# Layer 0 of a two-layer graph network: the norm of x and its fetch tested by place in the order instead of by a counter

## The chip, the core and the metric

The kernel runs on one core of a Trainium2 chip. The time is the device time of one execution in microseconds (us). The core has five engines that run beside each other, each with its own instruction queue: TensorE (PE, matmuls; PEld is its weight load), VectorE (DVE), ScalarE (ACT), GpSimd (POOL) and SyncE (SP, which here only issues DMAs). They wait for each other by semaphores.

## What is computed

For 16 batches of 1024 nodes with 128 features, two layers with a residual each. Layer 0 is three graph convolutions whose edge weights are the adjacency times the cosine of the node features; layer 1 first thins out the adjacency row by row ("dilation") and then runs three SAGE layers with batch norms on it.

```python
# layer 0, per batch
h = relu(layernorm(x))
for i in range(3):
    h = h @ W[i] + b[i]
    nh = h / max(norm(h), 1e-12)
    h = (adj * (nh @ nh.T)) @ h
    if i < 2: h = relu(h)
x = x + h
# layer 1, per batch
h = relu(layernorm(x))
adj_d = adj * keep          # keep: every sf-th neighbour of a row is removed, rows in sequence
for i in range(3):
    agg = (adj_d @ h) / max(sum(adj_d), 1)
    o = agg @ Wr[i] + h @ Wx[i] + bS[i]
    h = batchnorm(relu(o / max(norm(o), 1e-12)))       # statistics over all batches
x = x + concat(h1, h2, h3) @ Wl + bl
```

## The kernel before

The code hands a list of operations with tiles to a framework that allots the buffers of each pool and orders every engine's instructions ahead of time: an instruction may be placed earlier than in the text where its inputs and a buffer are free. The order on each engine is then fixed.

**Two stages.** The first, to about 1740 us, runs layer 0 of all batches and the dilation beside each other. The dilation (`dilation`, `dilate`, L519 to L718) goes through eight row blocks of 128 in two halves of eight batches: SP loads adjacency rows (`an`) and the transposed keep pattern (`kl`), ScalarE and VectorE make a 0/1 pattern, a few rounds on VectorE and TensorE settle which rows are cut, a running sum along each row on VectorE (L696) ranks the neighbours, and GpSimd issues the store of the keep pattern (`kp`). Layer 0 is a generator (`layer0`), and L740 to L743 draw from it so many steps for each finished part of the dilation. The second stage, from about 1740 us to the end, is layer 1's three SAGE layers (L773 on); the change does not touch it.

**Layer 0.** A batch is an object `Batch` with a counter `l` of the convolution it is in. The list `order` (L414) has 48 places: for each pair of batches a and b it reads a, b, a, b, a, b, so that six places make one pair. The loop at L443 goes through the places i; `now` is the batch of place i, `then` that of the next, `after` that of the one after next, and `ended` a batch whose third convolution was at the place before. Each place has eight steps s, one for a block row of the symmetric matrix:

- `products` (L310): the cosines of one block row by matmuls into `pg` (two PSUM banks), and VectorE multiplies them with the adjacency and its transpose (L334, L337) into `ew`.
- `turn` (L345): transposes of the second half of `ew`, copied back by ScalarE (L355).
- `sums` and `sums_back` (L357, L373): the matmuls that sum into `po`. They run LAG = 3 steps behind, so the last step of a convolution is summed at s = 2 of the next place. There `sums_back` copies `po` to `hT` and raises `l` (L391).

Beside these steps, `then` is prepared: at s = 0 its `norm` (only in its first convolution), at s = 3 the transposes of the normed x (`enter`, also only then), at s = 4 and 5 its product with the weights (`features`), and at s = 6 `turned` and `scaled`. At s = 5 the x of `after` is fetched if `after` is in its first convolution. For `ended`, x is fetched again at s = 1, the residual is added at s = 3 (`residual`), and at s = 5 the second layer's norm is taken (`next_layer`). The last batch's residual and second norm come after the loop (L769, L770).

**The norm and the fetch.** `fetch` (L252) is one DMA of 512 KB on SP into a buffer `xb`, of which there are two. `norm` (L256) takes a buffer `tt`, of which there are two also (shared with the residual's x2 and the second layer's h0), and calls `layernorm_relu` (L136): for each of eight chunks of 128 nodes a statistic and its aggregate on VectorE (L141, L142), then a root on ScalarE (L144), a reciprocal and a small product on VectorE (L145, L147), and eight activations on ScalarE (L149) that write the result. Both conditions that decide on them ask whether the counter is 0:

```python
                    if s == 5 and after and after.l == 0:
                        after.fetch()
                    if then:
                        new = then.l == 0
                        if s == 0 and new:
                            then.norm()
```

Of the kernel before, what the change touches and what calls it, by code (L numbers as in the profile page):

```python
# [46 lines left out]
def tile_adj_preln_d2(  # L47
# [122 lines left out]
    with ExitStack() as actx:  # L170
# [15 lines left out]
        after = pool1.tile([P, P], F16, name="after")  # L186
# [37 lines left out]
        def adj_piece(b, q):  # L224
            Nat[b, q] = nat = pool2.tile([P, NCH, P], F32, tag="nat", name=f"nat_{b}_{q}")
            nc.sync.dma_start(
                nat[:, : NCH - q, :], adj[b][q * P :, q * P : (q + 1) * P].rearrange("(c p) q -> p c q", p=P)
            )

        def adjT_tile(b, q):  # L230

            place, nat, row = adj_place(b, q), Nat.pop((b, q)), NCH - q
            if row > 1:
                nc.sync.dma_start(
                    place[:, row:, :].rearrange("p c q -> p (c q)"), adj[b][q * P : (q + 1) * P, (q + 1) * P :]
                )
            for c in range(0, row, CPH):
                n = min(CPH, row - c)
                pt = ps_sm.tile([P, CPH, P], F32, tag="sm", name=f"pt_a{b}_{q}_{c}")
                for i in range(n):  # L240
                    nc.tensor.transpose(pt[:, i, :], nat[:, c + i, :], ident)
                nc.scalar.activation(place[:, c : c + n, :], pt[:, :n, :], AF.Copy)
            nc.gpsimd.dma_start(adjT_d[b][q][:, q * P :], place[:, :row, :].rearrange("p c q -> p (c q)"))

        class Batch:
# [5 lines left out]
            def fetch(self):  # L251
                b = self.b  # L252
                self.xb = pool2.tile([P, NCH, D], F32, tag="xb", name=f"xb_{b}_{self.l}")
                nc.sync.dma_start(self.xb, x[b].rearrange("(c p) d -> p c d", p=P))
# [158 lines left out]
        batches = [Batch(b) for b in range(B)]  # L413
        order = [batches[b + i] for b in range(0, B, 2) for _ in range(3) for i in range(2)]  # L414

        def layer0():

            pieces = [((0, s), (1, SEQ[s])) for s in range(NCH)]
            for b in range(2, B):
                i = 6 * (b // 2) - 2 + b % 2
                for s in range(NCH):
                    at_ = min(2 * s + 2 - b % 2, 2 * NCH - 1)
                    pieces.append(((i + at_ // NCH, at_ % NCH), (b, SEQ[s])))
            pieces.sort()
            for s in range(NCH):
                adjT_tile(0, SEQ[s])
                if s < NCH - 2:  # L430
                    adj_piece(0, SEQ[s + 2])
                if s == 3:
                    order[0].enter(0)
                    order[0].enter(1)
                if 4 <= s < 4 + NHALF:
                    order[0].features(s - 4)
            order[0].turned()
            order[0].scaled()
            for (_, _), piece in pieces[:2]:
                adj_piece(*piece)  # L440
            yield 0.0
            behind, pieces_at = [], 0
            for i, now in enumerate(order + [None]):  # L443
                then = order[i + 1] if i + 1 < len(order) else None
                after = order[i + 2] if i + 2 < len(order) else None
                ended = order[i - 1] if i and order[i - 1] is not then else None
                if now:
                    now.begin()
                for s in range(NCH if now else LAG):
                    q = SEQ[s]  # L450
                    if now:
                        behind.append((now, s, *now.products(s)))
                        yield (NCH - q) * COLS
                    late = None
                    if len(behind) > LAG or not now:
                        late, s_, ew = behind.pop(0)
                        late.sums(s_, ew)
                        yield (NCH - SEQ[s_]) * COLS
                    if s > 0 and now or s == 0 and i:
                        b_, *of = behind[-2 if now else -1]  # L460
                        if now or s == 0:
                            b_.turn(*of)
                            yield (NCH - 1 - SEQ[of[0]]) * TURN
                    if late:
                        late.sums_back(s_, ew)
                        yield (NCH - 1 - SEQ[s_]) * COLS
                    if not now:
                        continue
                    while pieces_at < len(pieces) and pieces[pieces_at][0] == (i, s):
                        adjT_tile(*pieces[pieces_at][1])  # L470
                        pieces_at += 1
                        if pieces_at + 1 < len(pieces):
                            adj_piece(*pieces[pieces_at + 1][1])
                        yield (NCH - pieces[pieces_at - 1][1][1]) * TURN
                    if ended:
                        if s == 1:
                            ended.fetch()
                        if s == 3:
                            ended.residual()
                            yield NCH * TURN  # L480
                        if s == 5:
                            ended.next_layer()
                    if s == 5 and after and after.l == 0:
                        after.fetch()
                    if then:
                        new = then.l == 0
                        if s == 0 and new:
                            then.norm()
                        if s == 3 and new:
                            then.enter(0)  # L490
                            then.enter(1)
                            yield NCH * TURN
                        if s == 4 or s == 5:
                            then.features(s - 4)
                            yield CPH * COLS
                        if s == 6:
                            then.turned()
                            then.scaled()
                            yield NCH * TURN
# [24 lines left out]
        def dilate(k, half, exact):  # L524
# [166 lines left out]
            for i in range(BH + 1):  # L691
# [26 lines left out]
                yield 0.8  # L718

        units0 = layer0()  # L720

        blocks = NCH * (NCH + 1) // 2
# [50 lines left out]
    with ExitStack() as bctx:  # L773
# [134 lines left out]
        with ExitStack() as c1:  # L908
# [65 lines left out]
            then = fetch(0)  # L974
            for b in range(B):
# [4 lines left out]
                for q in range(NCH):  # L980
# [5 lines left out]
                    if q == 1 and b + 1 < B:  # L986
                        then = fetch(b + 1)
# [31 lines left out]
        def start2(l, b):  # L1019
            hT = normed(l, b, ab)  # L1020
            got = Sums(l, b, hT, CPH, 0, ps_a)
            for h, pp, a in project(l - 1, b, hT):
                if l == 1:
                    nc.scalar.activation(a, pp, AF.Copy)
                else:
                    nc.vector.tensor_tensor(a, pp, a, ALU.add)
            return got
# [12 lines left out]
        for l in (1, 2):  # L1040
            last = None
            then = start2(l, 0)
            for b in range(B):
                now = then
                for q in range(NCH):
# [5 lines left out]
                    if q == 2:  # L1051
                        if b + 1 < B:
                            then = start2(l, b + 1)
# [70 lines left out]
```

## Time and profile before

| | us |
|---|---|
| median of 3 runs | 3017.7 |
| lowest and highest run | 3014.06 and 3021.03 |
| the profiled execution | 3015.86 |
| its span | 3014.0 |
| first stage (layer 0 and dilation), to about | 1740 |

A profile is one execution. Its page gives each engine's busy time, groups of equal instructions with their number and mean duration, DMA issues, and the chain of work that ended last. Matmuls are pipelined and the ends of their records are modelled, so a busy TensorE is not one at its peak. A group's idle time is that of its engine just before it, put down to what came last. Where several instructions overlap in an engine's pipeline, the sum of their durations is more than the time that they take; the timeline shows the pace. The mean DMA rate over the span was 197 GB/s and the granted clock of TensorE 0.97.

### The profile page before, as it was taken

How to read it: one execution, taken by the hardware profiler on the slowest of the kernel's cores; microseconds unless marked ns; L12 is line 12 of the kernel's file. 1: busy time of each engine (PE TensorE's matmuls, PEld its weight loads, DVE VectorE, ACT ScalarE, POOL GpSimd, SP SyncE). 2: the span in 40 equal slices, each digit the busy share in tenths (PEclk: the TensorE clock that was granted, in tenths of full speed). 3: DMA queues.
4: the chain of work that ended last, by engine and by line, in shares of the span. 5: the costliest groups of instructions: out<-in, count | busy, mean ns of one | idle time of the engine just before them, and what ended most of it. 6: DMA issues, size and time to landing. Idle time of an engine off the chain costs nothing.

```text
span 3014.0 us, 52653 instructions
## 1 busy us (share of the span) xinstructions
PE 2723.9 (90%) x18915; PEld 2241.5 (74%) x18915; DVE 1974.0 (65%) x5234; ACT 1473.6 (49%) x4213; POOL 449.2 (15%) x604
## 2 busy tenths in 40 slices
PE   5989998998989989999999879988989999899996
PEld 4666676666666666676667678888879999899996
DVE  3878778877788779788885446656662323355555
ACT  6867658556556566566454323333333333333333
POOL 2112012111111121121111012222210101000010
PEclk9999999999999999999999989999999999999998
DMA  8456457355464485374440099999975555566663
GB/s 266 152 153 195 113 175 209 101 184 158 123 190 127 125 255 155 106 240 138 143 149 29 25 353 357 349 352 359 361 286 201 191 201 190 182 223 218 223 211 112
DMA packets 399664, 593.67 MB, mean 197 GB/s; under 512 B 85456, under 2 KB 283984, under 8 KB 399392
## 3 DMA queue, kind: packets, MB, share of 16 engines
q1 hardware_dynamic: 326640, 416.89, 43.6%
q0 software_dynamic: 38464, 156.07, 14.2%
q10 hardware_dynamic: 34288, 17.24, 1.9%
q8 instruction: 152, 2.49, 0.3%
q14 instruction: 120, 0.98, 0.1%
HBM read 411.83 MB, written 163.58 MB: 191 GB/s over the span
## 4 chain that ended last, share of the span: by engine, by line
PE 51%; DVE 21%; DMA 12%; ACT 7%; issue 6%; POOL 2%; SPq 0%; POOLq 0%; ACTq 0%; DVEq 0%; another core or an unknown queue 0%
PE agg L833 18%; PE po L365 6%; DVE rank L696 6%; PE pg L325 6%; PE po L379 4%; PE pw L806 4%; DVE ew L337 4%; DMA kl<-keep 3%; PE gt L354 2%; PE pp L1016 2%; DMA aT<-adjT 2%; PE pt_r L166 2%; PE pta L958 2%; ACT h L149 1%; PE pw L274 1%
## 5 line engine op out<-in xcount | busy, mean ns | idle before, releaser
L833 PE MATMUL agg<-hw,aT 128*128 128x128 f32 (+1 forms) x6144 | 763.5, 279 | 9.2 <-DVE aT L941 8.2
L833 PEld LDWEIGHTS agg<-hw,aT 128*128 128x128 f32 x6144 | 735.8, 195 | 16.4 <-DVE aT L941 11.2
L325 PE MATMUL pg<-nhT 128*128 128x512 f32 (+3 forms) x1152 | 458.1, 500 | 63.9 <-DVE ew L337 58.0
L365 PE MATMUL po<-ew,hS 128*128 128x512 f32 (+3 forms) x1152 | 456.5, 499 | 11.8 <-ACT hTo L388 8.9
L337 DVE TENSOR_TENSOR ew<-pg,adjA 128x768 f32<-128x768 f32 (+3 forms) x528 | 423.8, 824 | 5.0 <-DVEq L766 2.7
L379 PE MATMUL po<-ew,hS 128*128 128x128 f32 x2688 | 365.1, 276 | 0.0
L379 PEld LDWEIGHTS po<-ew,hS 128*128 128x128 f32 x2688 | 337.5, 192 | 35.0 <-issue 34.4
L355 ACT ACTIVATE ew<-gt 128x512 f32<-128x512 f32 (+1 forms) x480 | 208.8, 464 | 221.4 <-PE gt L354 218.5
L325 PEld LDWEIGHTS pg<-nhT 128*128 128x128 f32 x1152 | 188.7, 193 | 162.3 <-issue 108.7
L696 DVE TENSOR_TENSOR_SCAN rank<-patt 128x1024 f16<-128x1024 f16 x128 | 292.4, 2294 | 0.7
L365 PEld LDWEIGHTS po<-ew,hS 128*128 128x128 f32 x1152 | 195.7, 194 | 103.5 <-issue 71.9
L354 PEld LDWEIGHTS gt<-ident,ew 128*128 128x128 f32 x1344 | 167.9, 143 | 102.7 <-issue 69.5
L354 PE MATMUL gt<-ident,ew 128*128 128x128 f32 x1344 | 212.1, 277 | 6.1 <-ACT ew L355 4.8
L334 DVE TENSOR_TENSOR ew<-pg,adjA 128x128 f32<-128x128 f32 x384 | 106.5, 277 | 167.3 <-PE pg L325 133.7
L808 DVE TENSOR_TENSOR own<-pw,bs 128x256 f32<-128x256 f32 x192 | 79.1, 423 | 201.6 <-ACT hw L807 201.6
L881 POOL TENSOR_TENSOR o<-o,rn 128x512 f32<-128x512 f32 x96 | 103.8, 1081 | 702.2 <-DVE rn L880 454.5
L806 PE MATMUL pw<-wrx,hT 128*128 128x256 f32 x768 | 181.1, 390 | 10.3 <-ACT hT L1006 9.7
L860 DVE SCALAR_TENSOR_TENSOR o<-agg,invdeg,own 128x128 f32<-128x128 f32 x384 | 112.7, 343 | 116.8 <-PE agg L833 113.9
L959 ACT ACTIVATE aT<-pta 128x512 f32<-128x512 f32 (+3 forms) x160 | 70.6, 468 | 218.9 <-PE pta L958 216.4
L806 PEld LDWEIGHTS pw<-wrx,hT 128*128 128x128 f32 x768 | 146.1, 195 | 33.0 <-ACT hT L1006 10.5
L807 ACT ACTIVATE hw<-pw 128x256 f32<-128x256 f32 x192 | 71.0, 384 | 200.7 <-PE pw L806 149.8
L167 ACT ACTIVATE hR<-pt_r 128x512 f32<-128x512 f32 x96 | 55.7, 596 | 221.6 <-PE pt_r L166 221.6
(164 smaller groups left out, 4210.3 us busy)
## 6 DMA issues: line engine op xcount, KB each, us to landing
an<-in_adj_dram SPq DMA_DIRECT2D x128, 512.0 KB, 4.4
keep<-kp POOLq DMA_DIRECT2D x128, 256.0 KB, 3.3
kb<-keep SPq DMA_DIRECT2D x128, 256.0 KB, 5.6
aT<-adT SPq DMA_DIRECT2D x32, 960.0 KB, 4.6
aT<-adT SPq DMA_DIRECT2D x32, 832.0 KB, 4.7
xb<-in_x_dram SPq DMA_DIRECT2D x47, 512.0 KB, 4.3
aT<-adT SPq DMA_DIRECT2D x32, 704.0 KB, 4.0
aT<-adT SPq DMA_DIRECT2D x32, 576.0 KB, 3.4
```

Of the source, the lines that this page charges most:

```text
L325: nc.tensor.matmul(pg[:, :n, :].rearrange("p c q -> p (c q)"), lhsT=self.nhT[:, q * P : (q + 1) * P], rhs=self.nhT[:, (q + c) * P : (q + c ...
L334: nc.vector.tensor_tensor(ew[:, 0, :], pg[:, 0, :], place[:, 0, :], ALU.mult)
L337: nc.vector.tensor_tensor(both[0][:, :, off, :], pg[:, own:n, :].unsqueeze(1).to_broadcast([P, 2, n - own, P]), both[1][:, :, off, :], ALU ...
L354: nc.tensor.transpose(pt[:, i, :], ew[:, at + i, :], ident)
L355: nc.scalar.activation(ew[:, at : at + n, :], pt[:, :n, :], AF.Copy)
L365: nc.tensor.matmul(self.po[:, c * P : (c + n) * P], lhsT=self.hS[:, q, :], rhs=ew[:, c - q : c - q + n, :].rearrange("p c q -> p (c q)"), ...
L379: nc.tensor.matmul(self.po[:, q * P : (q + 1) * P], lhsT=self.hS[:, q + n, :], rhs=ew[:, NCH - 1 - q + n, :], start=False, stop=closes and ...
L696: nc.vector.tensor_tensor_scan(rank, pt[:, 1 : N + 1], pt[:, 2:], 0.0, ALU.add, ALU.add)
L806: nc.tensor.matmul(pw[:, i, :], lhsT=hT[:, 2 * h + i, :], rhs=wrx[:, l, :], start=True, stop=True)
L833: nc.tensor.matmul(self.place(c), lhsT=aT[:, blk, :], rhs=self.hw[:, source, :], start=False, stop=ends(c, source))
L860: nc.vector.scalar_tensor_tensor(self.o[:, c, :], self.place(c)[:, :P], invdeg[:, b, c : c + 1], self.own[:, c, :], ALU.mult, ALU.add,)
L881: nc.gpsimd.tensor_tensor(self.o[:, hc, :], self.o[:, hc, :], rn.unsqueeze(2).to_broadcast([P, CPH, D]), ALU.mult)
```

## The change

The function `first(i)` says whether place i of the order is the first convolution of its batch: places 0 and 1 of each six. The condition on the fetch asks it for the place of `after`, i + 2, and `new` asks it for the place of `then`, i + 1. The second condition on `new` (s = 3, `enter`) is written as before. The counter `l` stays; other code reads it.

```diff
         order = [batches[b + i] for b in range(0, B, 2) for _ in range(3) for i in range(2)]
+
+        def first(i):
+
+            return i % 6 < 2
 
...
-                    if s == 5 and after and after.l == 0:
+                    if s == 5 and after and first(i + 2):
                         after.fetch()
                     if then:
-                        new = then.l == 0
+                        new = first(i + 1)
                         if s == 0 and new:
                             then.norm()
                         if s == 3 and new:
```

## The prediction

> **What bounds the kernel now.** I read the page's busy table first, then the busy times by stretch, then what TensorE and VectorE waited for in the first 1740 us (where layer 0 and the dilation run), and last the chain of waits around one change of batch pair. The page says that no engine is full over the whole span:
>
> ```profile
> PE 2723.9 (90%) x18915; PEld 2241.5 (74%) x18915; DVE 1974.0 (65%) x5234; ACT 1473.6 (49%) x4213; POOL 449.2 (15%) x604
> ```
>
> The stretches tell more. A pair of batches takes some 212 us, and round each change of pair the norms, the residual and the transposes of new adjacency come together. Two such stretches (440 to 540, 1300 to 1420) and the two quiet ones after them; columns are length, then busy us of PE, PEld, DVE, ACT and POOL, the clock, the DMA share and GB/s:
>
> ```profile
> 440.00:540.00 100.00, 89.00 (x548) 64.56 (x547) 84.82 (x256) 75.01 (x202) 19.58 (x26) 0.98 0.65 194
> 540.00:650.00 110.00, 102.98 (x663) 75.14 (x662) 87.69 (x187) 60.06 (x152) 13.36 (x17) 1.00 0.40 120
> 1300.00:1420.00 120.00, 110.75 (x731) 82.02 (x730) 98.01 (x282) 79.34 (x231) 20.29 (x27) 1.00 0.62 191
> 1420.00:1510.00 90.00, 81.67 (x537) 58.60 (x536) 75.21 (x155) 40.95 (x117) 12.99 (x16) 1.00 0.41 125
> ```
>
> PE is busy nine tenths everywhere, DVE eight tenths, and near a change of pair ACT and the DMA are fuller too. What PE waits for most is VectorE: a product bank is freed only when the masking at L337 has read it. The lines are: engine and line, what it waited for, us in total, how often, the longest.
>
> ```profile
> PE pg L325 <- DVE ew L337: 58.0, 49, 2.5
> ...
> DVE ew L334 <- PE pg L325: 133.7, 87, 7.7
> ...
> DVE ln_st_l L141 <- DMA xb<-in_x_dram: 23.4, 6, 14.6
> ```
>
> So PE and DVE hand work to each other, and what stands before L337 in VectorE's order can cost PE time. In the first 1690 us I summed the chain of waits by engine: PE 695 us, DVE 521, DMA 181, ACT 164, issue 104. PE is the largest part but not the only one.
>
> The groups that the change cuts, in the first 1740 us (busy us, mean ns of one, idle time before):
>
> ```profile
> L149 ACT ACTIVATE h<-xb,ln_nmr_l,ln_rstd_l 128x128 f32<-128x128 f32 x256 | 106.9, 488 | 12.7 <-DVE ln_nmr_l L147 12.2 <-issue 0.2
> L141 DVE BATCH_NORM_STATS2 ln_st_l<-xb 128x6 f32<-128x128 f32 x256 | 63.9, 266 | 23.5 <-DMA xb<-in_x_dram 23.4
> L142 DVE BATCH_NORM_AGGREGATE ln_mv_l<-ln_st_l 128x2 f32<-128x6 f32 x384 | 58.5, 164 | 0.1
> ```
>
> 256 statistics of x are 32 norms of eight chunks each, for 16 batches: every batch is normed twice. The page's list of DMA issues has 47 fetches of x; 16 before a norm and 15 before a residual (the last batch's residual reads the x it has) make 31. The surplus follows from the code: l is raised at L391, when the lagged last step of a convolution is summed, and with LAG 3 that is at s = 2 of the convolution after it. L486 asks at s = 0, and L483 two places ahead at s = 5, both before the count has moved. So in each six of the order L486 is wrongly true at places 1 and 2, L483 at places 0 and 1: two norms and two fetches too many for each pair.
>
> **What the Trainium skill says.** "PSUM — Partial Sum Buffer", section "Engine vs sequencer instructions": ScalarE and VectorE queues are strict FIFO. The trace agrees: L337 waits its turn behind the norms, and PE's 58.0 us are the result. "Perfetto Trace Analysis", section "Identifying the Most-Contended Engine": matmul busy time is no good measure of how near TensorE is to its limit, the share of LDWEIGHTS is better. Here PEld is 65% at 440 to 540, against 94% at 2400 to 2500, so a PE that is 89% busy in the first stage has room. "VectorE: DVE Perf Modes", section "The TRN2 errata": small SBUF operations pay a fixed cost each; its formulas give an estimate of 186/0.96 = 194 ns for 128 elements on VectorE and 352/1.2 = 293 ns on ScalarE. The records are longer (266 and 488 ns) but overlap their neighbours; I use the pace in the timeline, which lies between.
>
> **The change part by part.** (1) Norms removed: 16, which the built program's order confirms: 288 instructions fewer on VectorE (16 x 18), 144 fewer on ScalarE (16 x 9), and 16 fetches fewer on SP. At 288.5 us one statistic and one aggregate follow each other every 0.26 us, so a norm costs VectorE 8 x 0.26 + 2 x 0.1 = 2.3 us, together 37 us. On ScalarE eight activations run in 3.17 us and the root adds 0.3, so 16 x 3.4 = 54 us. Both are engine time, not yet time of the kernel.
>
> (2) Fetches removed: 31 stay. 16 x 0.5 MB = 8 MB of 594 MB, 4.3 us each to land. Their bytes lie beside other work; what counts is their place. x has two buffers, and the superfluous fetch of one batch keeps the next pair's real fetch waiting, with SP's whole queue behind it. The timeline shows three fetches issued over 18 us (510.72 to 528.8), because each waits until ScalarE has read the norm before. The chain of waits goes through this place (start us, us, what):
>
> ```profile
> 506.90 3.08 ACT h L149 x8
> 509.98 0.74 ACT rank L705
> 510.72 5.47 DMA xb<-in_x_dram
> 516.18 0.02 issue
> 516.21 0.29 DVE ln_st_l L141
> 516.50 0.08 DVE ln_nmr_l L147
> 516.58 0.02 issue
> 516.60 2.80 ACT h L149 x7
> ```
>
> The first row is a superfluous norm, and the second norm there is another one; the fetch between them is that of the next pair's first batch, waiting for the buffer.
>
> (3) Moves. In the built order, the remaining instructions of TensorE, VectorE, ScalarE and SP stand nearly as before (on VectorE some 100 of 5367 change places with a neighbour, GpSimd's order is the same), so no stage is re-planned. One thing moves: the norm and the fetch of the next pair's first batch advance into the place of the first superfluous norm. For batch 4 the fetch stands after 99 other SP issues instead of 111, and its statistics after 351 other VectorE instructions instead of 372 to 383. Its buffer is free there, since the fetch that it replaces stood at the same place and landed in time. I price this at nothing: VectorE does the same work at that place as before. The cover is that equality; if the data came late, VectorE would stop for up to the 14.6 us of the longest such wait. No wait and no instruction is added. The loads queued behind the fetches on SP (adjacency rows, keep patterns, new tiles) stand a few us less.
>
> (4) The test by place itself is a Python expression and costs no instruction.
>
> Now the part on the path. Adding up the chain's pieces that belong to the leaving instructions gives 12 us on VectorE, and 5 to 13 us on ScalarE (by whether the first or the second superfluous norm is counted as the one replaced), and the two waits for x on the chain at a buffer's release, 5.5 and 3.6 us: 26 to 34 us, say 30. That is what goes if nothing else is nearly as late. But PE works beside it. A second sum bounds from below: over the six changes of pair (440 to 540, 650 to 750, 870 to 1010, 1090 to 1220, 1300 to 1420, 1510 to 1610) PE is busy 619.9 of 690 us (89.8%), in the six quiet stretches before or between them from 340 us on 533.6 of 580 (92.0%). Brought fully to 92.0%, the first would last 674 us, a gain of 16; over eight pairs 21. Only two of the six norms of a change leave, so a third of it, 7 us, is the low end. Between 7 and 30 I take 15 us, half of the chain's share, since both engines are still handed work by PE at every product. What is late next is PE with its own queue and the masking at L337. After 1740 us nothing changes.
>
> The profiled execution lasted 3015.86 us (span 3014.0 and 1.9 around it), near the median 3017.7. 3015.86 - 15 = 3000.9; from the median 3002.7. I forecast 3002.
>
> **Rivals.** A: hidden. PE's own stream sets the pace, and the removed work falls into VectorE's idle 20%. For it: PE is busy 9.7 of 10 us at 720 to 730 and 10 at 1590 to 1600, with such norms beside it. Against: VectorE is at 9.7 to 10 of 10 us at 280 to 300, 500 to 510 and 1140 to 1160, which is where the norms are. The time: gain 0 to 6, so 3012 to 3018.
>
> B: the whole chain goes, and the SP queue's relief frees the loads of the dilation behind it. For it: ScalarE waited 57.7 us for the adjacency rows and SP stood at 510, 723 and 1563 us for 18, 17 and 25 us. Against: at 530 to 560 us no load is waited for. Gain 24 to 40, about 30: 2988.
>
> C: slower. The advanced fetch holds SP's queue before its buffer is free, and adjacency rows and keep patterns behind it land late. Its place is the seven changes of pair. The longest wait of a fetch on SP is now 12.9 us; were such a hold added at each and a third of it to reach PE, 7 x 4.3 = 30 us are lost against 15 gained: 3033. It decides from 9 us per change on (7 x 3 = 21 = 15 + 6). Against it: in the built order the last reader of that buffer stands far ahead of the fetch.
>
> D: the change does nothing, as l was right already. 47 fetches and 32 norms exclude it.
>
> **How the numbers follow.** Main case, gain 7 to 24 us: 0.63. B 0.17, A 0.14, C 0.06. Faster by over 0.2% means more than 6 us, about what a measurement of this kernel can tell from no change: main case and B, 0.80. Within it: A, 0.14. Slower: C, 0.06. The range reaches into B and to A's upper part: 2986 to 3013.
>
> **What would show it.** 16 norms of x and 31 fetches; VectorE's busy time lower by about 37 us, ScalarE's by about 54; the wait of L325 for L337 under 58 us; the fetch at 510 us no longer three issues in 18 us; the first stage shorter by about 15 us and the rest unchanged. If the first stage loses as much VectorE time and is no shorter, A is right; if waits for an, kl or xb grow, C.

## The result and the profile after

| | before | changed |
|---|---|---|
| median of 7 runs, us | 3017.33 | 3007.02 |
| lowest and highest, us | 3014.06, 3021.03 | 2996.63, 3010.55 |
| the profiled execution (its span), us | 3015.86 (3014.0) | 3001.89 (2999.8) |

The ratio of the times is 0.9959, with a 95% interval of 0.9944 to 0.9975: the changed kernel is about 12.4 us faster (7.5 to 17). A second set of 7 runs, beside 12 of the kernel before, gave 0.9951 (0.9935 to 0.9968), 14.8 us. The mean granted clock of TensorE was 0.973 for both kernels in that second set, so a better clock is not what the change gained. The forecast was 15 us less, 3002.

The page's busy table of the changed kernel, and its line for the fetches of x:

```profile
PE 2712.1 (90%) x18915; PEld 2234.3 (74%) x18915; DVE 1942.6 (65%) x4946; ACT 1424.2 (47%) x4069; POOL 450.1 (15%) x604
...
xb<-in_x_dram SPq DMA_DIRECT2D x31, 512.0 KB, 4.8
```

DVE has 288 instructions fewer than before and 31 us less work, ACT 144 fewer and 49 us less. TensorE's 18915 matmuls are the same. The groups of the norm in the first 1740 us confirm 16 norms of x, 128 statistics of eight chunks each:

```profile
L149 ACT ACTIVATE h<-xb,ln_nmr_l,ln_rstd_l 128x128 f32<-128x128 f32 x128 | 54.3, 491 | 7.7 <-DVE ln_nmr_l L147 7.1 <-issue 0.4
L141 DVE BATCH_NORM_STATS2 ln_st_l<-xb 128x6 f32<-128x128 f32 x128 | 31.9, 265 | 20.3 <-DMA xb<-in_x_dram 20.3
```

The busy times by stretch, in the columns of before:

```profile
440.00:540.00 100.00, 90.45 (x572) 65.77 (x571) 83.53 (x223) 69.79 (x183) 18.52 (x24) 1.00 0.58 179
540.00:650.00 110.00, 101.47 (x640) 73.45 (x640) 88.42 (x186) 60.19 (x155) 14.82 (x19) 1.00 0.43 136
1300.00:1420.00 120.00, 111.28 (x768) 80.37 (x768) 95.93 (x232) 67.66 (x200) 18.58 (x22) 1.00 0.44 134
1420.00:1510.00 90.00, 82.53 (x536) 60.35 (x535) 73.74 (x166) 45.41 (x126) 14.55 (x20) 1.00 0.53 163
```

ACT has less to do at the changes of pair (75.0 to 69.8 and 79.3 to 67.7), and PE is a little busier there. The stretches are fixed times, and the work has moved against them by up to some 20 us, so they are no exact pairs. The waits in the first stage that the prediction had named (what waited, for what, us in total, times, longest):

```profile
DVE ew L334 <- PE pg L325: 149.4, 99, 6.4
...
PE pg L325 <- DVE ew L337: 60.3, 50, 3.7
...
DVE ln_st_l L141 <- DMA xb<-in_x_dram: 20.3, 3, 15.8
```

The first and the second have grown, not fallen. PE's wait for the masking at L337 was 58.0 us before. So the time went elsewhere.

**Where it went.** The copy at L388 closes each of the 48 places of the order, so its start marks the same point in both kernels:

| place | before, us | changed, us | difference |
|---|---|---|---|
| 5 (end of the first pair) | 266.0 | 266.9 | +0.9 |
| 18 | 726.0 | 716.0 | -10.0 |
| 24 | 947.5 | 932.7 | -14.8 |
| 47 (the last) | 1724.9 | 1707.2 | -17.7 |
| from there to the end of the span | 1289.1 | 1292.6 | +3.5 |

The first pair gains nothing, then the lead grows to 17.7 us. The 3.5 us after it lie within what this part varies: in the profiled executions of the other kernels below that leave the second stage alone it takes 1288 to 1299 us.

These are two single executions, and between executions of one kernel the time varies (the kernel before took 3005.8 to 3032.5 us in a set of 46 runs). Runs at a lower granted clock tend to be the longer ones: a straight line through these 46 gives 21 us for 0.01 of the clock. A part of the 17.7 us goes with the clock too. The first stage up to L388's last copy, in the kernel before, in the changed one, and in the repeat of the change (the last run below), in the columns of the prediction's table (the clock is the third number from the right):

```profile
0.00:1724.90 1724.90, 1550.93 (x9579) 1127.22 (x9579) 1319.24 (x3353) 1038.68 (x2776) 272.34 (x362) 0.98 0.51 153
0.00:1707.20 1707.20, 1540.98 (x9579) 1122.01 (x9579) 1288.64 (x3065) 989.41 (x2633) 272.58 (x362) 0.99 0.49 150
0.00:1717.20 1717.20, 1548.69 (x9579) 1125.62 (x9579) 1288.98 (x3065) 990.36 (x2633) 272.88 (x362) 0.98 0.49 149
```

PE's busy time for the same 9579 matmuls is 1550.9, 1541.0 and 1548.7 us. To three digits the clock is 0.980, 0.987 and 0.981, and busy time times clock is 1520.2, 1521.0 and 1519.4: nearly the same work, done at different clocks. So 9.9 of the 17.7 us go with the clock of these two executions, and the repeat, at nearly the clock of before, is 7.7 us ahead at this point.

What repeats better is the time in which PE is idle up to there: 174.0 us before (1724.9 - 1550.9), 166.2 changed, 168.5 in the repeat. Two of PE's waits fell most. Before:

```profile
PE pt_h L166 <- DVE x L402: 12.4, 8, 3.0
...
PE po L365 <- ACT hTo L388: 8.9, 9, 2.4
```

Changed:

```profile
PE pt_h L166 <- DVE x L402: 6.0, 5, 1.6
...
PE po L365 <- ACT hTo L388: 5.1, 6, 1.6
```

The first is the transposes of a normed x, waiting for the residual at L402 to read a bank of the same pool; the second is the next sum, waiting for ScalarE's copy at L388 to empty its bank. Together they fell by 10.2 us (21.3 to 11.1; 6.0 and 5.3 in the repeat), more than PE's whole idle time did, as others grew. The runs below show that they do not follow the time from kernel to kernel.

By place, most of the idle time did not go where the superfluous norms lay. I took the stretch from each L388 to the next and summed over the pairs by the position in the six. In the kernel before, the superfluous norms' activations lie in the stretches that end with positions 0 and 1. The norm that is needed of the next pair's first batch lies in those that end with 1 or 2; in the changed kernel it comes 20 to 70 us earlier (that of batch 10 starts at 921.5 us in place of 982.4), at position 0 in all pairs but one. In the stretches that end with positions 2 and 3, PE's idle time is 4.6 us less in the changed kernel and 5.0 in the repeat, which is most of what left. There PE waits less for the masking at L337 (27.0 to 21.2 us), and in those that end with position 0 it waits more for it (5.4 to 10.3). So the order, which moved with the change, may have a part in the gain.

SP's queue also shows what the prediction had looked for. Before, its wait for the buffer of a fetch, and the fetch at a change of pair:

```profile
SPq L254 <- ACT h L149: 69.9, 17, 8.1
```

```profile
510.72 18.07 SPq L254 DMA_DIRECT2D xb<-in_x_dram  x3
```

Changed:

```profile
SPq L254 <- ACT h L149: 32.8, 6, 8.6
```

```profile
507.94 0.38 SPq L254 DMA_DIRECT2D xb<-in_x_dram  x1
```

SP stands 37 us less at its fetches for this reason, and 82.1 us in place of 145.8 for all reasons together. Whether that, or the engine time of the norms, is what made the kernel faster, the two traces don't tell: both left at once. The experiments separate these two.

### The profile page after: what moved, and what is told of

Read it like the earlier page. It is cut to its first block, busy times and chain, and to the rows that moved or that the text cites. A ratio compares the mean times of both kernels' runs of the same rounds, so it can differ in the third digit from the quotient of the medians.

```text
span 2999.8 us, 52196 instructions
## 1 busy us (share of the span) xinstructions
PE 2712.1 (90%) x18915; PEld 2234.3 (74%) x18915; DVE 1942.6 (65%) x4946; ACT 1424.2 (47%) x4069; POOL 450.1 (15%) x604
## 4 chain that ended last, share of the span: by engine, by line
PE 50%; DVE 21%; DMA 13%; issue 6%; ACT 6%; POOL 2%; SPq 1%; ACTq 0%; POOLq 0%; DVEq 0%; another core or an unknown queue 0%
PE agg L837 16%; PE po L365 7%; PE pg L325 6%; DVE rank L700 6%; PE po L379 5%; PE pw L810 4%; DVE ew L337 4%; DMA aT<-adjT 3%; PE gt L354 2%; PE pp L1020 2%; DMA adT<-aT 2%; DMA kl<-keep 2%; PE pw L274 2%; PE pt_r L166 1%; DMA an<-in_adj_dram 1%
## 5 line engine op out<-in xcount | busy, mean ns | idle before, releaser
L325 PE MATMUL pg<-nhT 128*128 128x512 f32 (+3 forms) x1152 | 456.2, 498 | 68.8 <-DVE ew L337 60.3
L365 PE MATMUL po<-ew,hS 128*128 128x512 f32 (+3 forms) x1152 | 450.4, 494 | 10.7 <-ACT hTo L388 5.1
L337 DVE TENSOR_TENSOR ew<-pg,adjA 128x768 f32<-128x768 f32 (+3 forms) x528 | 423.9, 824 | 4.0 <-DVEq L770 3.0
L325 PEld LDWEIGHTS pg<-nhT 128*128 128x128 f32 x1152 | 188.8, 193 | 169.0 <-issue 115.8
L810 PEld LDWEIGHTS pw<-wrx,hT 128*128 128x128 f32 x768 | 146.7, 196 | 33.2 <-ACT hT L1010 10.3
```

What stands on the lines that cost most here:

```text
L325: nc.tensor.matmul(pg[:, :n, :].rearrange("p c q -> p (c q)"), lhsT=self.nhT[:, q * P : (q + 1) * P], rhs=self.nhT[:, (q + c) * P : (q + c ...
L337: nc.vector.tensor_tensor(both[0][:, :, off, :], pg[:, own:n, :].unsqueeze(1).to_broadcast([P, 2, n - own, P]), both[1][:, :, off, :], ALU ...
L365: nc.tensor.matmul(self.po[:, c * P : (c + n) * P], lhsT=self.hS[:, q, :], rhs=ew[:, c - q : c - q + n, :].rearrange("p c q -> p (c q)"), ...
L810: nc.tensor.matmul(pw[:, i, :], lhsT=hT[:, 2 * h + i, :], rhs=wrx[:, l, :], start=True, stop=True)
```

## The experiments

The theory: the norms' time on VectorE and ScalarE is what returns, a part of it, because PE's banks and the residual wait behind it. The rivals: the fetches' hold on SP's queue is what returns; or neither, and the first stage is shorter because the order of the work moved.

All runs start from the changed kernel. Each set of runs has its own runs of the kernel before, whose median ranged from 3013 to 3023 us, so the ratio to it is what is compared. "Excess" is (ratio - 0.9955) x 3018 us, with 0.9955 the mean of the change's two measurements; the error joins the two intervals. The last two columns are of the one profiled execution of each kernel, up to L388's last copy: PE's idle time, and the sum of its two waits shown above (for L402 and for L388).

| run | VectorE / ScalarE busy, against the change, us | median (runs) | ratio to before, 95% | excess, us | PE idle, us | the two waits, us |
|---|---|---|---|---|---|---|
| before | +31 / +49 | | 1 | 14 | 174.0 | 21.3 |
| the change | | | | 0 | 166.2 | 11.1 |
| e1_norm_once | +1 / -1 | 3005.21 (7) | 0.9949 (0.9925 to 0.9972) | -2 ± 8 | 166.2 | 14.6 |
| e2_work_twice | +31 / +47 | 3015.69 (22) | 0.9992 (0.9978 to 1.0006) | 11 ± 5 | 171.4 | 17.3 |
| e3_stats_twice | +30 / -1 | 3009.72 (17) | 0.9965 (0.9951 to 0.9979) | 3 ± 5 | 168.6 | 17.2 |
| e4_applies_twice | 0 / +45 | 3010.28 (13) | 0.9968 (0.9955 to 0.9981) | 4 ± 5 | 164.3 | 14.2 |
| f1_stats_four | +93 / +2 | 3022.48 (14) | 1.0005 (0.999 to 1.002) | 15 ± 6 | 174.7 | 8.7 |
| f2_applies_four | +1 / +139 | 3063.3 (5) | 1.0134 (1.0108 to 1.016) | 54 ± 8 | 197.9 | 12.2 |
| f3_work_thrice | +60 / +96 | 3032.96 (22) | 1.0037 (1.0026 to 1.0049) | 25 ± 5 | 185.2 | 25.1 |
| f4_norm_on_pool | +58 / -92 | 3041.84 (6) | 1.006 (1.0036 to 1.0083) | 32 ± 8 | 188.9 | 13.2 |
| g1_apply_on_dve | +57 / -91 | 2999.77 (6) | 0.9957 (0.9939 to 0.9974) | 1 ± 6 | 161.7 | 14.6 |
| g2_fetch_four | +2 / +1 | 3039.93 (6) | 1.0088 (1.0067 to 1.0109) | 40 ± 7 | 187.9 | 14.3 |
| g3_change_again | +1 / +1 | 2997.64 (7) | 0.9951 (0.9935 to 0.9968) | -1 | 168.5 | 11.3 |

**Norms once, fetches as before.** The norm is told by its place, the fetch still by the counter: 16 norms and 47 fetches.

```diff
-                    if s == 5 and after and first(i + 2):
+                    if s == 5 and after and after.l == 0:
```

> Half of the change: the norm of x once, the 16 superfluous fetches kept (47 fetches). Theory T1 (the gain is the engine time of the norms that leaves VectorE's and ScalarE's queues): most of the gain of about 12 us is here, 3004 to 3008 us. Theory T2 (the gain is SP's queue, which no longer waits for the release of x's buffers): no more than 3 us gained, 3014 to 3017 us. In both the wait of a fetch for ScalarE's read of x on SP should be short where no second norm reads x.

0.9949: the whole gain is there with the 16 superfluous fetches still issued. The interval allows that fetches cost up to some 6 us, but not that they are the gain. SP's standing at its fetches is 110.9 us here, so 29 of the 64 us that the change took off are back, and cost nothing that shows. Their bytes and their places on SP are hidden at this number. The order of the norms is the changed one here too: what this run shows is that the gain comes with the norms, not with the fetches.

**Fetches once, the norms' work twice in its place.** Each statistic and each activation of the first layer's norm runs twice, the second time with the same result. 31 fetches.

```diff
-    def layernorm_relu(pool, dst, src, nm):
+    def layernorm_relu(pool, dst, src, nm, stats=1, applies=1):
...
-        for c in range(NCH):
+        for c in [c for c in range(NCH) for _ in range(stats)]:
...
-        for c in range(NCH):
+        for c in [c for _ in range(applies) for c in range(NCH)]:
...
-                layernorm_relu(pool2, self.h, self.xb, f"l0_{b}")
+                layernorm_relu(pool2, self.h, self.xb, f"l0_{b}", stats=2, applies=2)
```

> The changed kernel with 31 fetches, but each first-layer norm does its statistics and its eight activations twice in place, with the same result: 37 us of VectorE and about 50 us of ScalarE put back, no fetch. T1: the gain is lost again, 3014 to 3020 us. T2: it stays, 3004 to 3009 us.

0.9992: with nearly the same engine time as before, and none of the superfluous fetches, the gain is gone. So this amount of work on VectorE and ScalarE costs about what the change returned. The two waits named above, in this kernel:

```profile
PE po L365 <- ACT hTo L388: 12.9, 10, 2.9
...
PE pt_h L166 <- DVE x L402: 4.4, 4, 1.6
```

The wait for the copy at L388 is back (8.9 before, 5.1 changed). That for the residual is not, and it is below the 12.4 us of before in every kernel of this study, doubled work or not; it seems to follow from the order, which all of them share with the change. But their sum does not follow the time: it is 17.2 us with only the statistics doubled, at an excess of 3, and 8.7 with four times the statistics, at an excess of 15. What does follow it, in order though not in size, is the whole of PE's idle time: kernels with a larger excess have more of it, but for steps within the errors.

The run is not the exact reverse of the change. It repeats the amount of the superfluous norms, not their positions, and the doubled work delays norms whose results the products need; the result of a superfluous norm was read by nothing. PE's idle time at positions 2 and 3 stays 5.6 us below that of before, and the stretches that end with positions 5 and 1, where most of the doubled norms stand, are 8.5 and 8.7 us longer than before, while those that end with 0 are 9.6 shorter. So the two runs show that the norms and not the fetches made the gain, and that their engine time has a price of that size. How much of the gain is this engine time and how much the new order (the third rival) is not shown: no run has the new order with the superfluous norms at their old places, or the old order without them.

**One engine at a time.** The same edit with stats=2, applies=1, and with stats=1, applies=2.

> The changed kernel with the 128 statistics and aggregates of the first-layer norms done twice in place (33 us of VectorE put back), the activations once. If VectorE's time is what counts: 3012 to 3018 us. If ScalarE's: at most 2 us slower than the changed kernel, 3005 to 3009 us.

> The changed kernel with the eight activations of each first-layer norm done twice in place (16 x 3.1 = 50 us of ScalarE put back), the statistics once. If ScalarE's time is what counts: 3012 to 3020 us. If VectorE's: at most 2 us slower than the changed kernel, 3005 to 3009 us.

0.9965 and 0.9968: either alone costs 3 or 4 us with an error of 5. The two add up to 7 ± 8 against 11 ± 5 for both, so neither that they simply add nor that they are worth more together is shown. Both medians lie between the two cases that I had named.

**Larger doses.** To come out of the noise: statistics four times, activations four times, both three times.

> The changed kernel with each statistic and aggregate of the first-layer norms done four times in place: three times 33 us, 100 us more of VectorE. Linear in VectorE's time from the run with twice the statistics (about 2 us for 33 us): 3013 to 3016 us. If VectorE alone carried the gain (10 us for 33): 3035 to 3045 us. If VectorE fills up only beyond some dose: more than three times the 2 us, above 3018 us.

> The changed kernel with the eight activations of each first-layer norm done four times in place: three times 50 us, 150 us more of ScalarE. Linear in ScalarE's time from the run with twice the activations (about 3 us for 50 us): 3014 to 3018 us. If ScalarE alone carried the gain (10 us for 50): 3035 to 3045 us.

> The changed kernel with statistics and activations of the first-layer norms done three times in place: 66 us of VectorE and 100 us of ScalarE more. If the two engines' times add up as single costs (2 and 3 us a dose): 3016 to 3019 us. If the two together cost more than the sum, as the run with both twice suggests (10 us a dose): 3024 to 3032 us.

VectorE: 93 us more cost 15, a sixth. Both engines: 156 us cost 25, a sixth as well, and twice what the single dose cost. So the price of this work, a sixth to a seventh, holds from one dose to two. For VectorE alone, 15 us is more than the 6 that the single dose had let me expect; with an error of 5 on that dose, a threshold is not shown. ScalarE isn't linear: 45 us cost 4, 139 us cost 54, more than either case that I had named. The waits of PE in the kernel with four times the activations say where:

```profile
PE pg L325 <- DVE ew L337: 60.0, 52, 3.6
...
PE pt_a L241 <- ACT adjA L242: 24.8, 5, 9.2
...
PE po L365 <- ACT hTo L388: 10.9, 12, 2.1
```

Before, PE waited 1.2 us for the second line. Its 24.8 us are five waits of up to 9.2 us: 32 activations in a row take 12.4 us at 488 us (the eight took 3.17), and the copy of the new adjacency at 500.4 us stands behind them. Not all of the 54 us is waiting: the mean granted clock of these runs is 0.968, against 0.972 for the kernel before beside them, and PE is busy for 1565.0 us with the 9579 matmuls. Why the clock is lower is not shown. With four times the statistics it is the masking that is late:

```profile
PE pg L325 <- DVE ew L337: 72.6, 52, 3.9
```

and with both three times the copy at L388:

```profile
PE po L365 <- ACT hTo L388: 22.5, 8, 7.5
```

That is the wait that the change had shortened from 8.9 to 5.1 us. PE's idle time follows the same order as the excess: 164.3 and 168.6 us for one engine's single dose, 171.4 for both, then 174.7, 185.2 and 197.9.

**More fetches.** The norms once, and three superfluous fetches at each place where the counter gave one: 79 in all, 48 too many.

```diff
-                    if s == 5 and after and first(i + 2):
-                        after.fetch()
+                    if s == 5 and after and after.l == 0:
+                        for _ in range(1 if first(i + 2) else 3):
+                            after.fetch()
```

> Norms once, and 48 superfluous fetches of x instead of 16 (79 in all). If fetches are hidden, as the run with the norm once and 16 superfluous fetches says: 3004 to 3011 us, as the changed kernel. If each superfluous fetch costs by SP's queue (the chain's two waits of 5.5 and 3.6 us): 9 us for 16 would be 27 us for 48, 3030 to 3036 us.

1.0088, 40 us over the change, more than I expected of either theory. SP's waits at the fetch with one superfluous fetch at a place (first experiment), and then with three:

```profile
SPq L254 <- ACT h L149: 41.6, 10, 10.3
SPq L254 <- DMA xb<-in_x_dram: 30.6, 13, 5.3
```

```profile
SPq L254 <- DMA xb<-in_x_dram: 90.0, 36, 4.9
SPq L254 <- ACT h L149: 43.6, 11, 10.3
```

SP's waits for an earlier fetch to land grew from 30.6 to 90.0 us, so 59 us of standing are added. VectorE then waits for x:

```profile
DVE ln_st_l L141 <- DMA xb<-in_x_dram: 43.5, 8, 14.6
```

against 20.3 (3 times) in the changed kernel. So fetches are not free as such: one at a place is covered, three are not. Whether SP's standing, the 25 MB more that move, or the lower granted clock (0.968 in the mean of these runs, 0.973 for the kernel before beside them) makes up the 40 us is not separated.

**Other engines for the norm.** Since a sixth of the norm's time shows, I tried whether what is left of it is better placed. The activation at L149, for the 32 norms of both layers, is done by VectorE in one kernel and as two operations of GpSimd in the other; the relu moves to the copies after the transposes in both.

```diff
-            nc.scalar.activation(
-                dst[:, c, :], src[:, c, :], AF.Relu, bias=nmr[:, c : c + 1], scale=rstd[:, c : c + 1]
-            )
+            nc.vector.tensor_scalar(
+                dst[:, c, :], src[:, c, :], rstd[:, c : c + 1], nmr[:, c : c + 1], ALU.mult, ALU.add
+            )
...
-                transposed(ps_sm, self.hT, self.h, f"h{self.b}", halves=(h,))
+                transposed(ps_sm, self.hT, self.h, f"h{self.b}", AF.Relu, (h,))
```

> The changed kernel with the eight activations of each of the 32 remaining norms done by VectorE (a product and a sum with columns, eight operations), the relu taken by ScalarE's copy after the transposes that it does anyway. ScalarE loses 100 us; VectorE gains some 32 x 8 x 0.2 = 50 us. By the doses: 50 us of VectorE cost about 7 us (13.8 for 100), 100 us of ScalarE less give 5 us at the small dose's price: 3007 to 3013 us. If the stretches of eight activations on ScalarE are what delays the copies that TensorE waits for, as the fourfold activations suggest: 2995 to 3003 us.

0.9957: no difference from the change. ScalarE is relieved of 91 us, VectorE gets 57. At the prices of the single doses the two about cancel (a sixth of 57 us more, 4 in 45 of 91 us less). The median, 2999.8, falls into the range that I had named for shorter stretches on ScalarE, but the kernel before took 3012.9 beside it, so this decides nothing.

```diff
-        for c in range(NCH):
-            nc.scalar.activation(
-                dst[:, c, :], src[:, c, :], AF.Relu, bias=nmr[:, c : c + 1], scale=rstd[:, c : c + 1]
-            )
+        for by, how in ((rstd, ALU.mult), (nmr, ALU.add)):
+            nc.gpsimd.tensor_tensor(dst, src, by.unsqueeze(2).to_broadcast([P, NCH, D]), how)
+            src = dst
...
```

> The changed kernel with the eight activations of each of the 32 remaining norms (both layers) replaced by two GpSimd operations over all chunks (a product and a sum with broadcast columns), the relu taken by ScalarE's copy after the transposes that it does anyway: 32 x 3.1 = 100 us of ScalarE less, 32 x 2 x 2 = 126 us of GpSimd more, which is 15% busy. If ScalarE's time counts at 3 us for 50: 6 us faster than the changed kernel, 3000 to 3003 us. If GpSimd's queue (stores of keep patterns and of adjacency behind the sums) or the norm's longer way counts: at or above 3010 us.

1.006, slower than before, although GpSimd is idle more than four fifths of the time. Its groups say that VectorE paid:

```profile
L149 POOL TENSOR_TENSOR h<-h,ln_nmr_l 128x1024 f32<-128x1024 f32 x32 | 64.9, 2027 | 6.2 <-DVE ln_nmr_l L147 2.6 <-DVE x L586 2.4
...
L147 DVE SCALAR_TENSOR_TENSOR ln_nmr_l<-ln_mv_l,ln_rstd_l 128x8 f32<-128x8 f32 x32 | 32.0, 1000 | 0.4
```

In the changed kernel the same small product at L147 takes 218 ns on average, so these 32 instructions alone last 25 us longer. VectorE stands at it for up to 3.1 us, with the maskings of the products behind it (PE's wait for L337's counterpart is 74.0 us against 60.3). Whether the norm's longer way through GpSimd adds to the loss is not separated. No version here is faster than the change.

**The change once more,** unchanged, beside the last two.

> The changed kernel once more, beside the runs that are compared with it: 3005 to 3010 us, a ratio of 0.9945 to 0.9970.

0.9951, in agreement with the first measurement. The median is below the 3005 to 3010 us that I had expected, as is that of the kernel before beside it, 3012.9.

## Why the prediction was right

The time came out at 3007.0 and 2997.6 in two sets of runs, around the forecast of 3002, and the main case (a gain of 7 to 24 us) is the one that happened. By its steps:

- **What bounds the kernel.** "PE and DVE hand work to each other, and what stands before L337 in VectorE's order can cost PE time": right in kind, as four times the statistics showed (60.3 to 72.6 us). But PE's 58.0 us of waiting for L337 cannot be put down to the norms that left, as the prediction did. It said that this wait would fall; it rose to 60.3 (60.0 in the repeat). What fell was PE's wait for ScalarE's copy at L388 and for the residual at L402, 21.3 to 11.1 us, which the prediction does not name. The share of the weight loads, 65% against 94%, was no sign of room either: a product at L325 takes 500 ns for a load of 193, the matmuls of the second stage at L833 279 for 195, so the share is lower in the first stage however full PE is.
- **(1) Norms removed.** Right: 288 and 144 instructions, VectorE's busy time lower by 31 us (37 forecast), ScalarE's by 49 (54). That the gain comes with the norms is shown by keeping the fetches (gain kept), and that engine time of this size costs as much by doubling the work (gain lost).
- **(2) Fetches removed.** "What counts is their place" was right for SP's queue, whose wait for the norm fell from 69.9 to 32.8 us, and for the group at 510 us. But it didn't reach the end: with the fetches kept the time was the same within 8 us. The 9 us that the chain's two waits for x put into the sum returned nothing that could be measured; up to some 6 us are not excluded.
- **(3) Moves.** Priced at nothing. The wait of the statistics for x is 20.3 us against 23.4, so no loss. The next pair's first norm did advance. But this term may have been wrong at nothing: PE's wait for the residual fell by 4 us or more in all kernels with the new order, and its idle time at positions 2 and 3 by about 5 us, also in the kernels with one double dose (4.5 to 5.6). No run has the moves alone, so what they return stays open. Rival C, an advanced fetch that holds SP's queue and makes the kernel slower, is excluded by the time and by SP's own waits. The wait for adjacency rows did rise a little, 57.7 to 64.8 us, and for keep patterns it fell, 36.8 to 21.7.
- **The path.** The chain's share of 30 us was the upper estimate; 12 to 15 us came, so the term was too large by half or more, and "half of the chain's share" met the size. The half was chosen between bounds and not derived, so that it met the size is luck in part. What the runs put in its place is a price: 80 us of busy time left two engines that are not full, and 14 us of them, a sixth, returned; the same sixth as when one or two doses of the work were added. The low end of 7 us, from closing a third of PE's gap between the changes of pair and the quiet stretches, was too low. PE is busy 631.1 of 690 us in the same six stretches now (91.5%, before 89.8), against 531.1 of 580 (91.6%) in the quiet ones; in the repeat it is 628.4 and 531.1. So the gap is nearly closed, not a third of it, with the reserve that the stretches have shifted against the work and that the busy share moves with the clock.
- **The first stage shorter by about 15, the rest unchanged.** 17.7 us in the profiled pair, of which 9.9 go with the clock, and 7.7 in the repeat (last copy at L388 at 1717.2). The rest is unchanged within its variation.
- **A and B.** A (0 to 6 us) lies outside the interval of both measurements. B (24 to 40 us) as well; its second half, loads freed by SP, has no support, as the fetches that were kept cost nothing measurable.

What stays open is how the 12 to 15 us divide between engine time and the new order, how the engine time divides between VectorE and ScalarE (3 and 4 us with an error of 5 each), and why PE's idle time explains only 5.5 to 8 us of them directly.

## What to carry to other kernels

Work that was taken off two engines of which neither is full returned as a fraction, here a sixth, and the same work added in one or two doses cost the same fraction; a longer unbroken stretch on ScalarE cost far more. No single wait told the fraction: the largest wait of the busiest engine rose, and two small ones that fell did not follow the time in the other kernels. PE's whole idle time up to a point that all kernels share did follow it, in order though not in size; its busy time has to be compared at the same granted clock. The chain of waits was an upper bound here; a transfer that appears on it at a buffer's release can still be covered. Where two things leave at once, put each back alone, and ask whether a third, the order, leaves with both.

## What was not expected of the hardware

With GpSimd's operations of 1.9 us beside it, VectorE's small product at L147 became slow, but not its statistics. The timeline of that kernel at its start (start us, us, engine, line):

```profile
22.36 0.48 DVE L141 BATCH_NORM_STATS2 ln_st_l<-xb 128x6 f32<-128x128 f32 x2
22.38 1.90 POOL L149 TENSOR_TENSOR h<-xb,ln_rstd_l 128x1024 f32<-128x1024 f32 x1 [13.37 <-DVE ln_mv_l L142]
22.75 0.16 DVE L142 BATCH_NORM_AGGREGATE ln_mv_l<-ln_st_l 128x2 f32<-128x6 f32 x1
22.84 0.26 DVE L141 BATCH_NORM_STATS2 ln_st_l<-xb 128x6 f32<-128x128 f32 x1
...
24.69 2.08 DVE L147 SCALAR_TENSOR_TENSOR ln_nmr_l<-ln_mv_l,ln_rstd_l 128x8 f32<-128x8 f32 x1
24.83 1.91 POOL L149 TENSOR_TENSOR h<-h,ln_nmr_l 128x1024 f32<-128x1024 f32 x1
```

The statistics run at 0.26 us beside the first GpSimd operation. L147 (of the next batch) ends at 26.77 us, with the second one (26.74), and takes 2.08 us in place of 0.17 some 2 us earlier. The Trainium skill, "SBUF — State Buffer", section "Who interferes with whom", states a lock between the two engines: a VectorE operation with two inputs in SBUF contends with a GpSimd operation that reads SBUF, and one of the two is blocked until the other is done; one with at most one SBUF input, outside the modes that use two ports, does not contend. The trace agrees for both: L147 has two such inputs, L141 one; and the maskings at L337, which read PSUM and SBUF, keep their 946 ns for 128x768 in both kernels. Which of the two came first the trace does not settle: L147's record starts 0.14 us before the GpSimd operation that it ends with, and spans on GpSimd are rough.
